# The last block of a mixture-of-experts kernel: four older tiles beside its sum, three tiles moved to the next stretch, additions held back

## The chip, the cores and the metric

The kernel runs on one core of a Trainium2 chip. The metric is the device time of one execution in microseconds (us), here the median of three. A profiled execution gives the trace; its span runs from the first instruction to the last.

## The reference

The input `x` is 16 sequences of 256 positions with 512 channels, 4096 rows in all. There are two layers.

```python
x = x + L0_ffn(L0_cond(x, ...))          # first layer
x = x + L1_ffn(L1_cond(x, cond), Wr, We, be)   # second layer

def L1_cond(x, w):      # a causal convolution of each channel by 16 taps
    return conv(x, w, padding=[(K - 1, 0)], feature_group_count=C)

def L1_ffn(x, Wr, We, be):                # 8 experts, the best two of each row
    w, sel = top_k(x @ Wr, 2)
    w = softmax(w)
    gate = one_hot(sel) weighted by w
    return sum(gate[..., e] * (x @ We[e] + be[e]) for e in range(8))
```

`L0_cond` adds one attended vector for each sequence and normalises; `L0_ffn` is a gated unit of width 2048 with weights and activations rounded to few values.

## The kernel before, in words

The rows are worked in four blocks of 1024 (`NB` = 4), each held as 128 partitions x 8 rows (`PH` = 8) x 512 channels. The first layer, `ffn`, goes through the 32 row groups in order: two products (L444), the gate on ScalarE and VectorE (L449, L450), a rounding (L456 to L462), the downward product (L486), and the sum into the block's tile (L491).

The second layer of a block has three parts:

- `conv` turns the block's channels (L670, copied out at L672) and multiplies them with Toeplitz blocks of the taps (L700), eight chunks of 24 matmul passes; VectorE copies each chunk back (L704). The taps come by L686.
- `route` turns the rows once more (L738, L740), computes the router's logits (L749), picks the best two (L754 to L768), ranks the rows of each expert (a matmul at L789) and gives each row a slot in that expert's region of a DRAM table (`slot`). Then, sixteen times, ScalarE makes a payload, the row times its gate (L810); GpSimd copies four numbers behind it (L811: where the result goes, and the gate) and writes the 128 rows to their slots with an indirect DMA (L812, "routed").
- `experts` takes tiles of 128 rows of one expert from that table. For each it loads the rows (L962), turns them on TensorE (L971), copies them out (L974 on ScalarE, or L976 on VectorE once all biases lie on the chip), multiplies with the expert's weights (L1021, eight passes) and adds the gated bias (L1041). The result `ye` goes out by GpSimd.

There are 71 tiles. A tile is full of one expert's rows, so blocks don't own tiles: after the routing of block n, the tiles that are surely full may run. Tiles 0 to 40 (`S_KEEP` = 41) hold rows of blocks 0 to 2 alone. Tiles 41 to 54 (`S_PURE` = 55) may hold rows of the last block and of older ones, tiles 55 to 70 rows of the last block alone.

Results leave in two ways. An *addition* (L935) is an indirect DMA that adds 128 rows into the output in DRAM; `Adds` makes each wait until the one before has landed. Results that are needed by the last block are instead *kept*: an indirect DMA writes them to the DRAM buffer `kept` (L1045). At the end `total` loads the last block's first-layer result (`x1`, L1069) and the two halves of `kept` (`y_kept`, L1075), adds them on VectorE (L1080) and writes the output (L1082). The `kept` loads wait for all kept writes.

The parts are generators, and `together` interleaves their steps in proportion to weights; a scheduler then sets each engine's order, largely by that order and by what is ready. GpSimd's queue takes indirect DMAs in order, and an instruction that waits holds all that follow.

The last pass of the main loop (n = 4) has an order of its own. Three tiles run with the first layer's last steps, with two result buffers in the pool `moe`. Then the first layer's memory is released and the pool `tail` takes its place: all biases (L1118), 10 tap buffers, 4 payload buffers, 6 row buffers and 6 result buffers. The last convolution and routing run beside tiles 28 to 40, and after them tiles 41 to 70 with a buffer pair of eight results each (`late_y`) for the first fourteen. `total` follows.

```python
                wanted = (s - s0 + 1) % 3 > 0 or s + 1 == s1
                left = 0 if s + 1 == s1 else max(len(held) - 1, 0)
            else:
                wanted, left = True, s + 1 < s1
```

These lines at the end of a tile say which held results are added now: before the last stage all but one, in the last stage two after three tiles.

Of the kernel before, what the change touches and what calls it, by code (L numbers as in the profile page):

```python
# [44 lines left out]
P = 128  # L45
# [10 lines left out]
def adaln_ffn_kernel(ctx: ExitStack, tc: tile.TileContext, t: dict, out: bass.AP):  # L56
# [27 lines left out]
    S_KEEP = TOP * PH * (NB - 1) - (NE - 1)  # L84
    S_PURE = TOP * PH * (NB - 1) + NE - 1
    RS = NT + P

# [573 lines left out]

    def conv(n, banks, pool, ahead):

# [15 lines left out]
        def load_taps(c):  # L679
            taps[c] = []  # L680
            for g in range(c * G4, (c + 1) * G4):
                taps[c].append(
                    pools[pool].tile([P, LAGS, P], F32, tag="taps", bufs=ahead, name="taps")
                    if c > 0 else conv_p.tile([P, LAGS, P], F32, tag="taps", bufs=5, name="taps")
                )
                nc.sync.dma_start(out=taps[c][-1], in_=t["toep"][:, g])  # L686
# [41 lines left out]

    def route(n, pool, pays):

# [74 lines left out]
        for p in range(PH):  # L805
            if p == PH // 2:
                tabs[n + 1] = tabulate(rhs)
            for i in range(TOP):
                pay = pools[pool].tile([P, ROW], F32, tag="pay", bufs=pays, name="pay")
                nc.scalar.activation(pay[:, 0:C], cv[:, p, :], AF.Identity, scale=ends[:, i, p, TOP + 1 : ROW - C])  # L810
                nc.gpsimd.tensor_copy(pay[:, C:ROW], ends[:, i, p, :])  # L811
                routings.append(nc.gpsimd.indirect_dma_start(  # L812
                    out=next(rv), out_offset=bass.IndirectOffsetOnAxis(ap=slot[:, i, p : p + 1], axis=0),
                    in_=pay[:, :], in_offset=None,
                ))
                yield
# [129 lines left out]

    def experts(s0, s1, tab, rows_in, written, pool, ahead, results):


        keeping = s0 >= S_KEEP  # L950
        why = "the table holds rows and experts of its own making"
        pool = pools[pool]
        got = {}
        held = []

# [11 lines left out]
        def turn(s):  # L967
# [4 lines left out]
            xT = moe.tile([P, KC, P], F32, tag="xT", name="xT")  # L972
            if biases is None:
                nc.scalar.copy(xT, xT_ps)  # L974
            else:
                nc.vector.tensor_copy(xT, xT_ps)  # L976
# [3 lines left out]
            if s < S_PURE:  # L980
# [3 lines left out]
                )  # L984
            if keeping:
                spare = part_no[:, 2 + s - s0 : 3 + s - s0]
                nc.vector.tensor_scalar(oi[:, 1:2], ends[:, TOP : TOP + 1], spare, None, ALU.min)
# [12 lines left out]

        for s in range(s0, min(s0 + ahead, s1)):
            load(s)
        turn(s0)
        yield
        late_y = None
        for s in range(s0, s1):
            if s + ahead < s1:
                load(s + ahead)
            if biases is None:
                load_bias(s)  # L1010
            if s + 1 < s1:
                turn(s + 1)
            yield
# [6 lines left out]
            for k in range(KC):  # L1020
# [4 lines left out]
                if k == 1:  # L1025
                    yield
            if keeping and s < S_PURE:
                if (s - s0) % PH == 0:
                    late_y = xp.tile([P, PH, C], F32, tag="x", name="late_y")
                ye = late_y[:, (s - s0) % PH, :]  # L1030
            else:
                ye = pool.tile([P, C], F32, tag="ye", bufs=results, name="ye")
# [9 lines left out]
            if s < S_PURE:  # L1042
                held.append((ye, oi))
            if keeping:
                keeps.append(nc.gpsimd.indirect_dma_start(  # L1045
                    out=next(keep_v), out_offset=bass.IndirectOffsetOnAxis(ap=oi[:, 1:2], axis=0),
                    in_=ye, in_offset=None,
                ))

                wanted = (s - s0 + 1) % 3 > 0 or s + 1 == s1  # L1050
                left = 0 if s + 1 == s1 else max(len(held) - 1, 0)
            else:
                wanted, left = True, s + 1 < s1
            while wanted and len(held) > left:
                y, i = held.pop(0)
                adds(y, i[:, 0:1], last_mm, *rows_in)
                rows_in = []
            yield

    def steps(s0, s1):  # L1060
        return 1 + 3 * (s1 - s0)

    def total():

        x1 = []
        for p in range(PH):
            tag, bufs = ("xg", 6) if p < 6 else ("pay", 4)
            x1.append(tail.tile([P, ROW], F32, tag=tag, bufs=bufs, name="x1")[:, 0:C])
            nc.sync.dma_start(out=x1[p], in_=x1_d[:, p, :])  # L1069
        halves = []  # L1070
        for i in range(TOP):
            halves.append(xp.tile([P, PH, C], F32, tag="x", name="y_kept"))
            rows = from_kept[i * P * PH : (i + 1) * P * PH, :].rearrange("(u p) c -> u p c", p=PH)
            for p in range(0, PH, 2):
                d = nc.sync.dma_start(out=halves[i][:, p : p + 2, :], in_=rows[:, p : p + 2, :])  # L1075
                for it in keeps:
                    tc.add_manual_dep(d.ins, it.ins.name, sync, reason="all results are there")
        for half in halves:
            for p in range(PH):
                nc.vector.tensor_tensor(x1[p], x1[p], half[:, p, :], ALU.add)  # L1080
                if half is halves[-1]:
                    nc.scalar.dma_start(out=out_x1_v[NB - 1][:, p, :], in_=x1[p])  # L1082

    def behind(n, banks, pool, pays, ahead):
        yield from conv(n, banks, pool, ahead)
        yield from route(n, pool, pays)
        if n + 2 < NB:
            load_x(n + 2, nc.sync)

    behind_steps = CONV_STEPS + ROUTE_STEPS  # L1090
    pools = {"moe": moe, "conv": conv_p}
    biases = None
    done = 0
    moe_steps, moe_part = 0, None
    for n in range(1, NB + 1):
        if n < NB:

            streams = [(behind_steps * 7 // 4, behind(n - 1, ps_c, "conv", 2, 5))]
            streams.append((STEPS, part(first_layer, STEPS)))
# [5 lines left out]
        else:  # L1105

            now = done + 3
            rest = behind(n - 1, ps_mm, "tail", 4, 10)
            next(rest)
            first = experts(done, now, tab, rows_in, written, "moe", 3, 2)  # L1110
            together((AHEAD, first_layer), (steps(done, now), first))
            done = now
            work.release()
# [8 lines left out]

            moe_steps, moe_part = steps(done, S_KEEP), experts(done, S_KEEP, tab, rows_in, written, "tail", 6, 6)
            done = S_KEEP
            head = CONV_STEPS + 1 + PH + 1
            for _ in range(2):
                next(rest)
            together((head - 4, part(rest, head - 4)), (3, part(moe_part, 3)))
            together((behind_steps - head, rest), ((moe_steps - 3) * 3 // 2, moe_part))
        end = NS if n == NB else TOP * PH * n - (NE - 1)  # L1130
        moe_steps, tab = steps(done, end), tabs[n]
        rows_in, written = list(stored[: PH // 2 * n]), list(routings)
        if n == NB - 1:
            continue
        moe_part = experts(done, end, tab, rows_in, written, *(("tail", 6, 6) if n == NB else ("moe", 3, 2)))
        done = end
    for _ in moe_part:
        pass
    total()


# [88 lines left out]
```

## Time and profile before

| | us |
|---|---|
| median of three runs | 1042.35 (1041.06 to 1042.97) |
| the profiled execution, its time | 1042.35 |
| its span | 1040.6 |
| TensorE busy in the span | 892.0 (86%) |
| VectorE, ScalarE, GpSimd busy | 582.0, 464.7, 330.0 |
| mean granted TensorE clock | 0.944 |

The shares are averages over stretches with different limits, so the last 270 us are read piece by piece: the first layer ends at 769, the last convolution at 819, the routed writes run from 850 to 881, tiles 41 to 70 from 891 to 1018, and the sum from 1021 on. In the lists of instructions a row gives start, duration, engine, line, operation, output and inputs, a count, and in brackets how long the engine had been idle and what ended that.

### The profile page before, as it was taken

How to read it: one execution, taken by the hardware profiler on the slowest of the kernel's cores; microseconds unless marked ns; L12 is line 12 of the kernel's file. 1: busy time of each engine (PE TensorE's matmuls, PEld its weight loads, DVE VectorE, ACT ScalarE, POOL GpSimd, SP SyncE). 2: the span in 40 equal slices, each digit the busy share in tenths (PEclk: the TensorE clock that was granted, in tenths of full speed). 3: DMA queues.
4: the chain of work that ended last, by engine and by line, in shares of the span. 5: the costliest groups of instructions: out<-in, count | busy, mean ns of one | idle time of the engine just before them, and what ended most of it. 6: DMA issues, size and time to landing. Idle time of an engine off the chain costs nothing.

```text
span 1040.6 us, 13445 instructions
## 1 busy us (share of the span) xinstructions
PE 892.0 (86%) x4456; PEld 503.3 (48%) x4456; DVE 582.0 (56%) x1274; ACT 464.7 (45%) x588; POOL 330.0 (32%) x407
## 2 busy tenths in 40 slices
PE   3687999699988799988798999879997999899890
PEld 1333443367743357653344766434546864344440
DVE  3899764876565966454578453734522353444244
ACT  3697764573587754456564515554521122000000
POOL 0245200632055221025524121452221037244550
PEclk9789998899999899999999999989998989899896
DMA  9961002855125134334431653354378358667676
GB/s 329 363 237 36 24 21 79 281 173 162 31 102 183 52 108 146 92 92 143 152 92 24 192 163 62 112 159 115 79 202 268 82 149 233 160 141 188 159 210 262
DMA packets 71932, 152.35 MB, mean 146 GB/s; under 512 B 9324, under 2 KB 26092, under 8 KB 71224
## 3 DMA queue, kind: packets, MB, share of 16 engines
q1 hardware_dynamic: 52440, 99.23, 29.2%
q0 software_dynamic: 17616, 47.59, 18.8%
q10 hardware_dynamic: 1808, 4.68, 1.3%
q8 instruction: 36, 0.59, 0.2%
q14 instruction: 32, 0.26, 0.1%
HBM read 97.29 MB, written 54.18 MB: 146 GB/s over the span
## 4 chain that ended last, share of the span: by engine, by line
PE 43%; DMA 15%; DVE 13%; ACT 11%; issue 10%; POOL 6%; SPq 1%; DVEq 0%; ACTq 0%; POOLq 0%
PE acc_ps L1021 12%; PE acc_ps L444 9%; PE acc_ps L700 7%; DMA routed<-pay,slot 5%; PE acc_ps L486 4%; DMA out<-late_y,oi 3%; PE acc_ps L749 3%; ACT hq L456 3%; DVE h L450 2%; PE acc_ps L971 2%; ACT hq L462 2%; DMA xt<-in_x 2%; PE acc_ps L738 1%; ACT pay L810 1%; ACT hqT L476 1%
## 5 line engine op out<-in xcount | busy, mean ns | idle before, releaser
L1021 PE MATMUL acc_ps<-we,xT 128*128 x568 | 271.6, 614 | 7.1 <-DVE xT L976 6.7
L444 PEld LDWEIGHTS <-qT 128*128 128x128 bf16 x1024 | 99.7, 99 | 153.0 <-issue 50.2
L450 DVE SCALAR_TENSOR_TENSOR h<-acc_ps,c,h 128x512 f32<-128x512 f32 x128 | 95.2, 746 | 120.4 <-PE acc_ps L444 66.9
L1021 PEld LDWEIGHTS acc_ps<-we,xT 128*128 128x128 f32 x568 | 107.1, 198 | 109.6 <-issue 95.4
L444 PE MATMUL acc_ps<-w2q,qT 128*128 128x512 fp8e4 x512 | 135.9, 387 | 16.1 <-DVE h L450 9.3
L444 PE MATMUL acc_ps<-w1q,qT 128*128 128x512 fp8e4 x512 | 135.5, 383 | 9.8 <-ACT h L449 5.5
L486 PE MATMUL acc_ps<-w3q,hqT 128*128 128x512 fp8e4 x512 | 127.3, 399 | 10.3 <-ACT hqT L476 4.9
L935 POOL DMA_INDIRECT out<-ye,oi x41 | 65.8, 1606 | 208.0 <-PE acc_ps L1021 140.4
L449 ACT ACTIVATE h<-acc_ps,c 128x512 f32<-128x512 f32 x128 | 86.3, 681 | 91.8 <-PE acc_ps L444 91.3
L700 PE MATMUL acc_ps<-taps,xT 128*128 128x128 f32 x768 | 95.9, 282 | 12.4 <-DVE ye L1041 5.5
L700 PEld LDWEIGHTS acc_ps<-taps,xT 128*128 128x128 f32 x768 | 91.2, 196 | 15.8 <-DVE ye L1041 5.7
L486 PEld LDWEIGHTS <-hqT 128*128 128x128 bf16 x512 | 51.4, 102 | 77.4 <-issue 21.7
L812 POOL DMA_INDIRECT routed<-pay,slot x64 | 67.3, 1052 | 48.0 <-ACT pay L810 15.3
L462 ACT ACTIVATE hq<-h,neg_magic 128x2048 bf16<-128x2048 f32 x32 | 64.1, 2002 | 34.4 <-DVE h L461 31.8
L458 DVE TENSOR_REDUCE hmx<-h 128x1 f32<-128x2048 f32 x32 | 73.0, 2282 | 0.6
L810 ACT ACTIVATE pay<-xt,ends 128x512 f32<-128x512 f32 x64 | 45.5, 721 | 58.4 <-DMA routed<-pay,slot 56.1
L456 ACT ACTIVATE hq<-h 128x2048 bf16<-128x2048 f32 x32 | 61.2, 1912 | 20.0 <-DVE h L450 19.8
L476 ACT COPY hqT<-acc_ps 128x1024 bf16<-128x1024 bf16 x64 | 61.6, 1009 | 15.4 <-PE acc_ps L474 11.8
L390 POOL TENSOR_TENSOR y<-xt,pb 128x512 f32<-128x512 f32 x30 | 42.3, 1428 | 54.6 <-ACT q L418 37.3
L1041 DVE SCALAR_TENSOR_TENSOR ye<-biases,xe,acc_ps 128x512 f32<-128x512 f32 x29 | 21.7, 747 | 67.8 <-PE acc_ps L1021 37.3
L704 DVE COPY xt<-acc_ps 128x512 f32<-128x512 f32 x32 | 32.6, 1030 | 39.8 <-PE acc_ps L700 39.8
L971 PEld LDWEIGHTS acc_ps<-ident,xg 128*128 128x128 f32 x284 | 36.0, 147 | 35.4 <-issue 24.1
(194 smaller groups left out, 1112.6 us busy)
## 6 DMA issues: line engine op xcount, KB each, us to landing
taps<-in_toep SPq DMA_DIRECT2D x128, 192.0 KB
xg<-routed SPq DMA_DIRECT2D x71, 258.0 KB
xt<-in_x SPq DMA_DIRECT2D x16, 512.0 KB
we<-in_We POOLq DMA_DIRECT2D x8, 1024.0 KB
bias<-in_be SPq DMA_DIRECT2D x28, 256.0 KB
out<-xt SPq DMA_DIRECT2D x12, 512.0 KB
st<-in_w1T SPq DMA_DIRECT2D x4, 1024.0 KB
st<-in_w2T SPq DMA_DIRECT2D x4, 1024.0 KB
```

The costliest lines, as they stand in the source:

```text
L444: nc.tensor.matmul(acc[-1], lhsT=qTs[i][:, k, bass.ts(j, P)], rhs=wq[:, k, bass.ts(f, 512)], start=(k == 0), stop=(k == KC - 1),)
L449: marks["silu", m] = nc.scalar.activation(h, acc[0], AF.Silu, scale=c1[:, j : j + 1])
L450: marks["glu", m] = nc.vector.scalar_tensor_tensor(h, acc[1], c2[:, j : j + 1], h, ALU.mult, ALU.mult)
L456: nc.scalar.activation(hq, h, AF.Square, accum_out=hss)
L458: nc.vector.tensor_reduce(hmx, h, AX.X, ALU.max, apply_absolute_value=True)
L462: nc.scalar.activation(hq, h, AF.Identity, bias=neg_magic)
L476: nc.scalar.copy(hqT, hT_ps)
L486: nc.tensor.matmul(o_ps, lhsT=hqT[k // half][:, k % half, :], rhs=w3q[:, k, :], start=(k == 0), stop=(k == KF - 1),)
L700: nc.tensor.matmul(cv_ps[:, g, :], lhsT=xT[:, g, at : at + P], rhs=mine[g][:, lag, :], start=(lag == 0), stop=(lag == LAGS - 1),)
L812: routings.append(nc.gpsimd.indirect_dma_start(out=next(rv), out_offset=bass.IndirectOffsetOnAxis(ap=slot[:, i, p : p + 1], axis=0), in_=p ...
L935: d = nc.gpsimd.indirect_dma_start(out=next(add_v), out_offset=bass.IndirectOffsetOnAxis(ap=idx, axis=0), in_=ye, in_offset=None, compute_ ...
L1021: last_mm = nc.tensor.matmul(e_ps, lhsT=xT[:, k, :], rhs=we[:, bass.ds(e, 1), k, :].rearrange("p o f -> p (o f)"), start=(k == 0), stop=(k ...
```

## The change

Tiles get an order list (`seq`) instead of a range, and `S_LAST` = `S_KEEP` - 4 = 37.

- Block 2's time in the first layer has 13 tiles (9 to 21) instead of 16; the three beside the first layer's end are 22 to 24; the last routing has 25 to 36; the last stage has 41 to 70 and then 37 to 40.
- `total` becomes a generator. It is started after tile 70, and its sum is interleaved with what is left of the four older tiles, whose additions come last. The output is written from SP's queue instead of ScalarE's.
- The list of held results is shared by all calls. In the last routing the results of tiles 31 to 36 are held, and added in the last stage, two after three tiles as before.
- In the last routing, the convolution and the logits come before tile 25's matmuls in the written order, with only that tile's rows turned ahead; before, one tile was interleaved with them and the following ones ran with a larger weight.
- Taps, payloads and `x1` of the last block share 12 buffers. The four numbers behind a payload are copied by ScalarE in the last routing. The turned rows are copied by ScalarE in the last stage. The biases of the three tiles at the first layer's end are loaded a tile earlier.

```diff
+    S_LAST = S_KEEP - 4
...
+    def row_of_tail(name):
+        return pools["tail"].tile([P, ROW], F32, tag="row", bufs=12, name=name)
...
-                nc.gpsimd.tensor_copy(pay[:, C:ROW], ends[:, i, p, :])
+                if pool == "tail":
+                    nc.scalar.copy(pay[:, C:ROW], ends[:, i, p, :])
+                else:
+                    nc.gpsimd.tensor_copy(pay[:, C:ROW], ends[:, i, p, :])
...
-    def experts(s0, s1, tab, rows_in, written, pool, ahead, results):
+    held = []
+    def experts(seq, tab, rows_in, written, pool, ahead, results):
...
-            if biases is None:
+            if biases is None or seq[0] >= S_KEEP:
                 nc.scalar.copy(xT, xT_ps)
...
-            if s + 1 < s1:
-                turn(s + 1)
+            for ready in seq[i + 1 : i + 2]:
+                turn(ready)
+                if biases is None and len(seq) == 3:
+                    load_bias(ready)
...
-                wanted = (s - s0 + 1) % 3 > 0 or s + 1 == s1
-                left = 0 if s + 1 == s1 else max(len(held) - 1, 0)
+                wanted = (s - S_KEEP + 1) % 3 > 0 or s + 1 == NS
+                left = 0 if s + 1 == NS else max(len(held) - 1, 0)
+            elif s >= S_LAST:
+                wanted, left = True, 0
             else:
-                wanted, left = True, s + 1 < s1
+                wanted, left = s < S_LAST - results, s not in (seq[-1], S_LAST - results - 1)
...
     def total():
...
+        yield
         for half in halves:
             for p in range(PH):
                 nc.vector.tensor_tensor(x1[p], x1[p], half[:, p, :], ALU.add)
                 if half is halves[-1]:
-                    nc.scalar.dma_start(out=out_x1_v[NB - 1][:, p, :], in_=x1[p])
+                    nc.sync.dma_start(out=out_x1_v[NB - 1][:, p, :], in_=x1[p])
+                if p % 2:
+                    yield
...
-            now = done + 3
+            first = [done + i for i in range(3)]
...
-            moe_steps, moe_part = steps(done, S_KEEP), experts(done, S_KEEP, tab, rows_in, written, "tail", 6, 6)
-            done = S_KEEP
+            moe_steps, moe_part = steps(seq), experts(seq, tab, rows_in, written, "tail", 6, 6)
             head = CONV_STEPS + 1 + PH + 1
             for _ in range(2):
                 next(rest)
-            together((head - 4, part(rest, head - 4)), (3, part(moe_part, 3)))
-            together((behind_steps - head, rest), ((moe_steps - 3) * 3 // 2, moe_part))
+            next(moe_part)
+            for _ in range(head - 4):
+                next(rest)
+            together((behind_steps - head, rest), (moe_steps - 1, moe_part))
...
+            end = TOP * PH * n - (NE - 1) - (3 if n == NB - 2 else 0)
...
-    for _ in moe_part:
-        pass
-    total()
+    seq = [*range(S_KEEP, NS), *range(S_LAST, S_KEEP)]
+    moe_part = experts(seq, tab, rows_in, written, "tail", 6, 6)
+    for _ in range(steps(range(S_KEEP, NS))):
+        next(moe_part)
+    last_sum = total()
+    next(last_sum)
+    for _ in range(7):
+        next(moe_part)
+    together((PH, last_sum), (steps(range(S_LAST, S_KEEP)) - 7, moe_part))
```

## Prediction, made before the changed kernel ran

> **What bounds the kernel now.** I read the page's slices, then busy time in stretches cut where the last block changes its work, then the queues of GpSimd (POOL) and VectorE (DVE) in order of time, and last the chain of waits. A tile is one pass of `experts`, 0 to 70. The stretches (length; busy us and instructions of PE, PEld, DVE, ACT, POOL; clock; DMA share; GB/s):
>
> ```profile
> 740.00:770.00 30.00, 30.00 (x136) 14.97 (x135) 12.69 (x25) 11.56 (x13) 7.74 (x8) 1.00 0.49 109
> 770.00:801.00 31.00, 23.64 (x134) 16.77 (x132) 4.00 (x10) 4.49 (x8) 4.67 (x3) 0.99 0.96 306
> 850.00:881.00 31.00, 31.00 (x99) 15.55 (x98) 16.30 (x60) 8.62 (x12) 24.06 (x32) 1.00 0.88 259
> 974.00:1018.00 44.00, 38.50 (x106) 17.92 (x104) 14.63 (x32) 0.00 (x0) 23.47 (x22) 0.92 0.66 177
> 1025.00:1031.00 6.00, 0.00 (x0) 0.00 (x0) 5.94 (x10) 0.00 (x0) 0.00 (x0) 0.50 1.00 393
> ```
>
> TensorE (PE) bounds the first layer's end, is idle for 7.4 us at the start of the last convolution and 5.5 us late in the last stage, and has nothing in the final 22 us, where the DMA engines are full. The timeline shows the idle time at the convolution:
>
> ```profile
> 782.99 0.75 DVE L1041 SCALAR_TENSOR_TENSOR ye<-bias,xe,acc_ps 128x512 f32<-128x512 f32 x1 [8.84 <-DMA out<-ye,oi]
> 791.01 0.75 DVE L1041 SCALAR_TENSOR_TENSOR ye<-bias,xe,acc_ps 128x512 f32<-128x512 f32 x1 [7.28 <-DMA out<-ye,oi]
> 800.33 0.75 DVE L1041 SCALAR_TENSOR_TENSOR ye<-bias,xe,acc_ps 128x512 f32<-128x512 f32 x1 [7.79 <-DMA out<-ye,oi]
> 801.13 5.49 PE L700 MATMUL acc_ps<-taps,xT 128*128 128x128 f32 x24 [5.48 <-DVE ye L1041]
> ```
>
> Results of tiles 25, 26 and 27 wait for a free one of two buffers, that is for an addition (L935) to land; behind them on DVE stand the convolution's copies (L704), and PE waits for their banks. The end of the chain of waits:
>
> ```profile
> 974.03 5.68 DMA out<-late_y,oi
> 980.48 2.86 DMA out<-late_y,oi
> 987.86 4.80 DMA kept<-ye,oi
> 1017.84 2.71 DMA kept<-ye,oi
> 1020.82 4.01 DMA y_kept<-kept
> ```
>
> Additions run one by one; the kept writes (L1045) queue behind them on POOL, tiles wait for buffers that those writes hold, and after the last kept write come its landing, the loads of `y_kept` and the sum.
>
> **The change, part by part** (span 1040.6 us; the profiled run took 1042.35, so 1.75 lies outside; that is also the median). Positions are from the built queues of both kernels.
>
> *First layer.* Before its last L486, PE's queue holds 24.5 tiles now and 22 after. A tile costs 3.87 us (four L971 at 0.44 in all, eight L1021 at 3.44). PE is busy for 68.4 of 700 to 770, but 32.6 of the 40 us before it, where half a tile also leaves. I take 2 tiles, **-8** (bounds 0 and 2.5 x 3.87 = -9.7). Call E the moment of the last L491, 768.90 now, 760.9 after.
>
> *Additions and the convolution.* The wait for buffers stays: tile 24 will need addition 22, as tile 27 needs addition 25. An addition is queued after the next tile's last matmul, and its buffer is free when it lands. Counting matmuls back from E in the new queue, addition 18 can go at E-15, and 19 and 20 follow at 7.3 us (766.37 to 773.69), so 20 goes at E-0.4; at 8.1 (the mean of the five gaps from 766.37 to 806.82, while the DMA engines are full) 21 goes at E+7.7 and 22 at E+15.8, which lands near E+24. Now tile 27 comes at E+31.4. So the convolution's copies come **-7** nearer to E (0 if DMA bounds this stretch; -9, which is 5.5 and 1.6 idle and 2 of slow clock after it). The bias that tile 23 needs is queued ahead of the taps instead of among them; now the taps stand behind such a bias from 769.9 to 774.10. PE ends its tiles at E+11.7 and three chunks (2.7 and 0.4 of transposes each) by E+21, so this wait remains the last. The last convolution matmul moves from 818.9 to about 803.9.
>
> *Logits to the first routed write.* PE has 3.25 tiles between convolution and rank matmul (L789), 2.5 after: 0.75 x 3.87, **-2.9** (0 to -3.9).
>
> *The sixteen routed writes.* Four additions stand between the first and the last of them, now and after: what is held back is tiles 31 to 36, not these. Their gaps are 6.6 to 7.4 us (853.98, 860.56, 867.70, 875.05), longer than three writes and an addition (3 x 1.28 + 1.9 = 5.7). So the four-element copies moved from POOL to ACT (0.2 us each, on an ACT queue with 22 us free in 31) shorten nothing: **0** (-3, POOL bound; +1). Nor do the twelve shared row buffers: ACT waited 8.1 us (at 854.19) for one of four, but POOL never more than 1.2 in this stage. On SP four loads of the sum's first operand now stand ahead of tile 41's rows; their buffers come free with the payloads of writes 4 to 7, before the last write, which those rows await anyway: 0.
>
> *Start of the last stage.* Tile 36 ends at 885.2 - 15 - 3.87 = 866 (tile 40 now ends at 885.2; after the convolution 12 tiles follow instead of 13), the first rows land at 887.07 - 17.9 = 869, so PE idles again. Now 3.9 us pass from landing (887.07) to the matmul (890.95), since DVE first does two old results. ACT does the copy in the new order, free of them: about 1.6 (transposes and a copy of 0.58 by L974). **-2.3** (0 to -4).
>
> *Thirty tiles.* Tile 41's result to tile 70's took 897.13 to 1016.82, 119.7, against 29 x 3.87 = 112.2. The 7.5 lost are waits for kept writes behind additions. The new queue spreads two additions over three kept writes up to the last: 11.4 us (5.72 each, 922.63 to 996.96) against 11.6 of tiles. I take **-6** (0 to -7.5).
>
> *The end.* From the last kept write, K, 22.8 us passed to the end (1017.84 to 1040.6). Now four tiles run there and four additions close POOL's queue. Tile 37's result comes 3.6 us after K (3.87 after tile 70's, and 0.75 long), and each addition waits for the one before. DMA share is 1.00 to K+18, so I price the first two at that 8.1, the third at 7, the last at 5.7, landing within: 3.6+8.1+8.1+7+5.7 = 32.5, say 32: **+9.2**. Bounds: all at 5.7 behind DVE's results, 27.5 (+4.7); all at 9.1 (773.69 to 801.03), 40 (+17). On DVE the result of tile 38 stands behind three sums that wait for `y_kept` (K+7 and 2 us), and those of 39 and 40 behind six and five more; they are ready by K+20, before their additions' turns. SP takes the output's eight issues at 0.33, behind loads that are done: nothing.
>
> The Trainium skill ("DMA: Bandwidth & Descriptors", Anatomy of one DMA) gives a GpSimd DMA about 2 us and its bytes at 436 GB/s, 2.6 us for an addition's 256 KB by my estimate. By it four additions would hide beside the sum, and the end would cost nothing. The same page (Issuing engines are not separate DMA queues) speaks against the change: all issuers share the same engines. By bytes alone, 1 MB at 400 GB/s adds an estimated 2.6 us. The trace's spacing of 5.72 and more decides against both.
>
> Sum: -8 -7 -2.9 +0 -2.3 -6 +9.2 = -17.0; span 1023.6, time 1025.4.
>
> **Rivals.**
>
> *DMA bounds the convolution.* In 770 to 801 the share is 0.96 at 306 GB/s, 9.5 MB of biases, taps and rows, and the same bytes move after. Then the term of -7 is 0: 1032.4. Against: PE waited for taps only 0.3 us there.
>
> *Additions pace the last stage (slower).* Between the last routed write and the last kept write stand 21 additions, and each now also stands behind kept writes that wait for tiles. At 5.72 they take 120 us from about 862 and end 8 us before the tiles, so they decide from 5.72 + 8/21 = 6.1 on, and cost 21 us per us beyond. At 6.8 (mean of the routed stage) the last kept write is 15 later: 1040, no change; at 7.35 (its longest) 26 later: 1051.5. From 6.9 on it is slower than now. For it: the two paces differ by 0.2 us in 11.6. Against: the same neighbours gave 5.72.
>
> *The end stays short.* If the additions run at 5.72 there, +4.7 replaces +9.2: 1020.9.
>
> *It does not do what it says.* The additions between routed writes stay four; that is in the sum at nothing.
>
> **Numbers.** The sum's case 0.58, short end 0.12, DMA-bound convolution 0.17, pacing additions 0.13 (of which 0.09 beyond 1044.4, 0.03 near no change and 0.01 below). About 0.2% (2.1 us) is what a measurement can tell here. So faster 0.58 + 0.12 + 0.17 + 0.01 = 0.88, less 0.01 to the same side for a near miss: 0.87; same 0.04; slower 0.09. Term errors of about 4, 4.5, 2, 2, 2, 3 and 6 give some 10 about 1025.4; with the DMA case the range runs from 1013 to 1038, leaving out the pacing case and a stroke of luck in all terms.
>
> **What would show it.** Right: last L491 near 761; tile 24's result near 785 after a wait for an addition; last convolution matmul near 804 (818.9 now); first routed write near 832, last near 862; L974 on ACT in the last stage; last kept write near 992 with additions 5.7 apart; four additions 6 to 8 us apart after it, the last thing to land. Wrong: the additions' spacing over 6.1 in the last stage, PE waiting for taps, or a chain that ends with the output's writes and not with an addition.

## The result, and the profile after

Over twenty timed executions of each kernel the changed one has a median of 1037.26 us and the one before 1042.61 us. The ratio is 0.9946, with a 95% interval of 0.9927 to 0.9965: faster by 5.6 us, between 3.6 and 7.6. The forecast was 17. The profiled execution of the changed kernel took 1038.07 us, its span 1036.3 (before 1042.35 and 1040.6).

I read the stretches first (length; busy us and instructions of PE, PEld, DVE, ACT, POOL; clock; DMA share; GB/s). Lines of the changed kernel are numbered a little higher: L492 is the sum behind the downward product (L491 before), L1035 the tile's matmuls, L1055 its result, L947 the addition, L1059 the kept write, L1097 the sum.

```profile
740.00:770.00 30.00, 29.75 (x136) 15.15 (x134) 12.56 (x25) 12.05 (x14) 7.10 (x6) 1.00 0.55 123
770.00:801.00 31.00, 21.96 (x129) 16.99 (x128) 6.64 (x13) 3.41 (x6) 5.52 (x6) 0.94 0.96 297
881.00:1001.00 120.00, 120.00 (x370) 59.05 (x369) 37.94 (x109) 18.40 (x32) 59.58 (x49) 0.99 0.75 181
1001.00:1036.00 35.00, 12.14 (x35) 5.48 (x33) 12.92 (x22) 1.17 (x2) 8.38 (x6) 0.71 0.75 231
```

The last stage is now full: PE is busy for all of 120 us. The stretch at the convolution is not better but a little worse: 22.0 us of PE in 31 instead of 23.6, at the same DMA share of 0.96. The timeline of that stretch (start, duration, engine, line, and in brackets idle time and what ended it) shows why:

```profile
765.57 1.56 POOL L947 DMA_INDIRECT out<-ye,oi  x1 [5.10 <-DVE ye L1055]
779.87 1.55 POOL L947 DMA_INDIRECT out<-ye,oi  x1 [12.74 <-PE acc_ps L675]
787.11 1.56 POOL L947 DMA_INDIRECT out<-ye,oi  x1 [4.98 <-DVE ye L1055]
794.59 0.75 DVE L1055 SCALAR_TENSOR_TENSOR ye<-bias,xe,acc_ps 128x512 f32<-128x512 f32 x1 [4.78 <-DMA taps<-in_toep]
795.28 1.55 POOL L947 DMA_INDIRECT out<-ye,oi  x1 [6.61 <-DMA out<-ye,oi]
```

With E the last L492 (766.31), addition 20 goes at E-0.7, as forecast (E-0.4). Then comes a gap of 14.3 us where the sum had 8.1, and tile 24's result comes at E+28.3 instead of E+24. The label "taps" on that result is the case of a wait for several semaphores: its buffer came free when the addition of 787.11 landed, for which the next addition waited too (last line). What PE waited for between 755 and 815, and what held SP's queue before it issued the next taps (what waits, for what: us, times, longest):

```profile
PE acc_ps L675 <- DVE xT L988: 5.6, 1, 5.6
PE acc_ps L983 <- DMA xg<-routed: 3.2, 1, 3.2
SPq L692 <- DMA biases<-in_be: 6.8, 1, 6.8
```

The 5.6 us are VectorE's queue: a copy of turned rows stands there behind tile 24's result and two of the convolution's copies. The 3.2 us are rows that came late. They are issued on SP's queue behind the taps, and that queue stood still for 6.8 us, until the 2 MB load of all biases had landed (for 5.0 us in the kernel before, where PE waited for no rows).

The end of the chain of waits, and below it the additions behind the last kept write (1001.50):

```profile
1001.50 3.06 DMA kept<-ye,oi
1004.96 6.56 DMA y_kept<-kept
1012.16 0.74 DVE ye L1055
1021.11 5.70 DMA out<-ye,oi
```

```profile
1003.68 1.60 POOL L947 DMA_INDIRECT out<-ye,oi  x1 [1.22 <-DVE oi L994]
1013.18 1.75 POOL L947 DMA_INDIRECT out<-ye,oi  x1 [7.90 <-DVE ye L1055]
1021.11 2.34 POOL L947 DMA_INDIRECT out<-ye,oi  x1 [6.19 <-DVE ye L1055]
1027.56 1.54 POOL L947 DMA_INDIRECT out<-ye,oi  x1 [4.11 <-DMA out<-ye,oi]
```

Where before the chain ended with `y_kept`, the sum and the output, it now ends with additions. One thing in these two traces misleads. Up to the twentieth of the 32 downward sums the queues of both kernels hold the same order, yet the changed kernel reached that point at 493.0 and the one before at 488.5. Fourteen experiments and one more trace of the kernel before gave more traces of most stages, since each experiment leaves most of the order as it is. So the stages can be compared by means. A row takes the traces whose experiment leaves its stage as it is; the run with the 2 MB load in small pieces is in none (in the stages that it leaves alone it would widen no range by more than 0.1 us), and the run that holds no results back is not in the last two (its end took 35.8).

| stage | before, 2 traces | changed order (range; traces) | measured | forecast |
|---|---|---|---|---|
| start to 20th downward sum | 491.1 | 491.6 (488.5 to 495.1; 12) | +0.5 | 0 |
| to the last downward sum, E | 280.3 | 274.5 (272.1 to 278.2; 12) | -5.8 | -8 |
| to the last convolution matmul | 49.0 | 48.3 (46.0 to 50.6; 7) | -0.7 | -7 |
| to the first routed write | 29.3 | 25.6 (24.0 to 28.1; 7) | -3.7 | -2.9 |
| to the last routed write | 29.7 | 31.4 (30.6 to 31.9; 7) | +1.7 | 0 |
| to the last kept write, K | 139.0 | 128.5 (127.6 to 129.3; 6) | -10.5 | -8.3 |
| to the end | 22.6 | 34.5 (34.2 to 34.9; 6) | +12.0 | +9.2 |

The stages behind the first row sum to -7.0, which the interval of the timings (-7.6 to -3.6) holds. Two rows make most of the missing ten: the convolution (6.3) and the end (2.8). The two traces of before lie 3.6 us apart in the row to the first routed write and 2 us apart in the rows to the last convolution matmul and to K, so these rows are uncertain by about as much; the convolution's -0.7 can't be told from nothing.

### The profile page after: what moved, and what is told of

It reads as the page before. It is cut to its first block, busy times and chain, and to the rows that moved or that the text cites. A ratio compares the mean times of both kernels' runs of the same rounds, so it can differ in the third digit from the quotient of the medians.

```text
span 1036.3 us, 13485 instructions
## 1 busy us (share of the span) xinstructions
PE 886.6 (86%) x4456; PEld 501.1 (48%) x4456; DVE 568.0 (55%) x1243; ACT 484.1 (47%) x635; POOL 326.5 (32%) x391
## 4 chain that ended last, share of the span: by engine, by line
PE 50%; DVE 13%; DMA 12%; ACT 10%; issue 8%; POOL 6%; SPq 1%; DVEq 0%; POOLq 0%; ACTq 0%
PE acc_ps L1035 18%; PE acc_ps L445 9%; PE acc_ps L706 7%; DMA routed<-pay,slot 5%; PE acc_ps L487 5%; PE acc_ps L755 3%; PE acc_ps L983 3%; ACT hq L457 2%; DVE h L451 2%; DMA taps<-in_toep 2%; DMA xt<-in_x 2%; ACT hq L463 2%; POOL r L131 1%; PE acc_ps L744 1%; POOL y L391 1%
## 5 line engine op out<-in xcount | busy, mean ns | idle before, releaser
L1035 PE MATMUL acc_ps<-we,xT 128*128 x568 | 264.6, 602 | 1.6 <-ACT h L450 1.4
L1035 PEld LDWEIGHTS acc_ps<-we,xT 128*128 128x128 f32 x568 | 104.5, 193 | 99.5 <-issue 92.6
L487 PE MATMUL acc_ps<-w3q,hqT 128*128 128x512 fp8e4 x512 | 130.9, 408 | 9.7 <-ACT hqT L477 4.8
L947 POOL DMA_INDIRECT out<-ye,oi x41 | 66.1, 1613 | 218.2 <-PE acc_ps L1035 124.7
L986 ACT COPY xT<-acc_ps 128x512 f32<-128x512 f32 x59 | 34.4, 585 | 160.5 <-PE acc_ps L983 146.9
L706 PEld LDWEIGHTS acc_ps<-taps,xT 128*128 128x128 f32 x768 | 90.3, 195 | 10.1 <-issue 2.2
L391 POOL TENSOR_TENSOR y<-xt,pb 128x512 f32<-128x512 f32 x30 | 42.3, 1427 | 54.4 <-ACT q L419 36.4
L1055 DVE SCALAR_TENSOR_TENSOR ye<-biases,xe,acc_ps 128x512 f32<-128x512 f32 x32 | 23.9, 747 | 63.2 <-PE acc_ps L1035 58.3
```

What stands on the lines that cost most here:

```text
L487: nc.tensor.matmul(o_ps, lhsT=hqT[k // half][:, k % half, :], rhs=w3q[:, k, :], start=(k == 0), stop=(k == KF - 1),)
L706: nc.tensor.matmul(cv_ps[:, g, :], lhsT=xT[:, g, at : at + P], rhs=mine[g][:, lag, :], start=(lag == 0), stop=(lag == LAGS - 1),)
L947: d = nc.gpsimd.indirect_dma_start(out=next(add_v), out_offset=bass.IndirectOffsetOnAxis(ap=idx, axis=0), in_=ye, in_offset=None, compute_ ...
L1035: last_mm = nc.tensor.matmul(e_ps, lhsT=xT[:, k, :], rhs=we[:, bass.ds(e, 1), k, :].rearrange("p o f -> p (o f)"), start=(k == 0), stop=(k ...
```

## The experiments

Each was timed beside the kernel before; the changed kernel stands at 0.9946 on that scale. 0.001 is 1.04 us. A difference between two such ratios is uncertain by some 3 to 4 us, so the traces decide about stages, and the ratios about large effects only.

**Own result buffers at the convolution.** Two of the three tiles take payload buffers that are idle there.

```diff
-                ye = pool.tile([P, C], F32, tag="ye", bufs=results, name="ye")
+                if len(seq) == 3 and i < 2:
+                    ye = conv_p.tile([P, ROW], F32, tag="pay", bufs=2, name="ye")[:, 0:C]
+                else:
+                    ye = pool.tile([P, C], F32, tag="ye", bufs=results, name="ye")
```

> Two of the three tiles beside the first layer's end get result buffers of their own, so none of their results waits for an addition that is still under way; the same bytes move. Theory (additions bound the start of the last convolution, as predicted, and one of them took 13.6 us there): the result of tile 24 comes about 14 us after the last L492 instead of 28.3, PE's idle time before the convolution's banks goes, the last convolution matmul comes 5 to 8 us nearer to the last L492 than the 48.6 us of the changed kernel, and the time falls by about 5 us. Rival (the DMA bytes of biases, taps and rows bound this stretch): PE waits for taps or rows instead, the last convolution matmul stays within 2 us of 48.6, the time within 1 us.

Ratio 0.9916 [0.9887, 0.9946], 3 us under the changed kernel. The convolution ends at E+44.5. VectorE's timeline around it, E being 762.61, and what PE waited for:

```profile
767.35 0.75 DVE L1058 SCALAR_TENSOR_TENSOR ye<-bias,xe,acc_ps 128x512 f32<-128x512 f32 x1 [3.99 <-PE acc_ps L1035]
771.22 0.75 DVE L1058 SCALAR_TENSOR_TENSOR ye<-bias,xe,acc_ps 128x512 f32<-128x512 f32 x1 [3.12 <-PE acc_ps L1035]
785.58 0.17 DVE L990 COPY xe<-xg 128x4 f32<-128x4 f32 x1 [13.61 <-DMA xg<-routed]
786.49 0.74 DVE L1058 SCALAR_TENSOR_TENSOR ye<-bias,xe,acc_ps 128x512 f32<-128x512 f32 x1
```

```profile
PE acc_ps L983 <- DMA xg<-routed: 3.8, 1, 3.8
```

Two results now follow PE at once. The third, tile 24's, stands on VectorE behind a small copy of tile 25's first row data, whose load came late, at E+23. That is neither the theory's E+14 nor the rival's unchanged convolution. So additions were the last wait, as the prediction said, but a second one lay just 4 us under it: rows that stand on SP's queue behind the taps and the 2 MB load (SP waits 6.7 us for that load here too).

**The 2 MB load of biases later.** It is issued behind half of the convolution, by a dependency on that copy.

```diff
-            nc.scalar.dma_start(
-                out=biases.rearrange("p e c -> p (e c)"),
...
             for _ in range(head - 4):
                 next(rest)
+            d = nc.scalar.dma_start(
+                out=biases.rearrange("p e c -> p (e c)"),
...
+            tc.add_manual_dep(d.ins, copied[-4].ins.name, sync, reason="after half of the convolution")
```

> The 2 MB load of all biases is issued behind half of the last convolution instead of ahead of it (some taps then stand behind rows on SP's queue); the bytes in all are the same. Theory (that load, beside the taps, is what stretches one addition to 13.3 to 13.8 us in all five traces): this addition takes 7 to 9 us, tile 24's result comes about 22 us after the last L492 instead of 28, the last convolution matmul 3 to 6 us sooner, time -4. Rival (taps and rows alone fill the DMA engines): the addition still takes 12 us or more, tile 24 stays at 27 to 29, time within 1.5 us.

Ratio 0.9902 [0.9863, 0.9941]; the convolution ends at E+43.8. The gap behind addition 20 is 8.8 us, instead of 13.5 to 14.3 in the nine traces that have the changed order there and the load in its place. PE waits for no rows there either:

```profile
768.22 1.56 POOL L949 DMA_INDIRECT out<-ye,oi  x1 [5.62 <-DVE ye L1057]
777.01 1.55 POOL L949 DMA_INDIRECT out<-ye,oi  x1 [7.22 <-issue]
```

**Taps later, biases in place.** The edit before had also moved some taps on SP's queue, so the taps were tried by themselves.

```diff
-                nc.sync.dma_start(out=taps[c][-1], in_=t["toep"][:, g])
+                d = nc.sync.dma_start(out=taps[c][-1], in_=t["toep"][:, g])
+                if pool == "tail" and c > 0:
+                    order_behind(d, bias_loads[-1])
```

> Of the changed kernel only SP's order at the last convolution: the taps behind the first chunk's are issued after the bias of tile 24, which waits for a buffer; the 2 MB load of all biases stays at the end of the first layer. The late load of the biases had also moved half of ten taps behind that bias, so it did not tell which of the two stretched the addition issued 0.4 us before the last L492. Theory A (the 2 MB of biases do): it takes 12 us or more again. Theory B (it is the burst of taps): 7 to 9 us, though the taps come later. Either way PE may wait for taps, so the time is open: -4 to +4.

Ratio 0.9954 [0.993, 0.9978]. The gap is 13.8 us again:

```profile
762.08 1.56 POOL L949 DMA_INDIRECT out<-ye,oi  x1 [5.16 <-DVE ye L1060]
775.90 1.55 POOL L949 DMA_INDIRECT out<-ye,oi  x1 [12.26 <-PE acc_ps L675]
```

So the 2 MB load stretches that addition, not the burst of taps. The load hangs on E in both kernels and begins within 0.1 us of it; what moved is the additions. In the kernel before, this load began at 768.94, 2.6 us after one addition (766.37) and 4.8 us ahead of the next (773.69), and the gaps behind them were 7.3 and 10.0. In the changed order it begins 0.3 to 0.8 us after the addition in all nine traces. The DMA queues between 755 and 815 in the changed kernel (packets, MB, share of 16 engines) let one suspect the size of its packets:

```profile
q1 hardware_dynamic: 6192, 9.72, 50.5%
q0 software_dynamic: 937, 1.69, 18.2%
q10 hardware_dynamic: 144, 2.10, 9.3%
```

q10 holds the biases, 14.6 KB a packet on average; q0 the indirect DMAs, 1.8 KB. The Trainium skill ("DMA: Bandwidth & Descriptors", Queues, rings and completion order) has each DMA engine take turns between queues by whole packets, which would make a small packet wait for a large one each time.

**The same load in small pieces.**

```diff
-            nc.scalar.dma_start(
-                out=biases.rearrange("p e c -> p (e c)"),
...
+            for e in range(NE):
+                nc.scalar.dma_start(out=biases[:, e, :], in_=t["be"][e, :].partition_broadcast(P))
```

> Of the changed kernel only the form of the 2 MB load: eight DMAs of 256 KB, one per expert, instead of one; they start at the same place (the second to seventh behind ScalarE's copy for tile 23). In the trace of the changed kernel this load goes in 144 packets of 14.6 KB (2.10 MB / 144), the additions in packets of 1.8 KB (1.69 MB / 937). Theory P (the addition shares each DMA engine with that load turn by turn, a packet each, and each of its small packets waits for a large one): the addition issued 0.4 us before the last L492 takes 8 to 10 us instead of 13.6, tile 24's result comes 4 us sooner, the last convolution matmul 44 to 45 us after the last L492, time -4, though the same bytes move. Theory B (the bytes themselves hold it up): 12 us or more, convolution 47 to 50, time unchanged.

The load went in 1152 packets of 1.8 KB, the gap was 11.2 us, tile 24 came at E+27.4, the convolution ended at E+46.4; ratio 0.9922 [0.9884, 0.9961]. That is between the two theories. But three of the eight pieces were issued only at E+10.3, E+11.7 and E+14.1, when tile 23's result (E+10.1) had shown that the addition was down, so fewer bytes met it as well. What the packets and what the bytes contribute to the five us stays open, and the rule about turns is neither refuted nor shown.

**The end: results ahead of the sums.** All four older tiles' results stand before the first sum on VectorE.

```diff
+                a = nc.vector.tensor_tensor(x1[p], x1[p], half[:, p, :], ALU.add)
+                tc.add_manual_dep(a.ins, made[-1].ins.name, in_turn, reason="an engine's order")
```

> On VectorE the four older tiles' results stand ahead of all sixteen sums; nothing else moves. Theory (the final additions wait in part for results that stand behind sums): the second addition comes about 2 us and the fourth about 2 us sooner, and from the last kept write to the end pass 31 to 33 us instead of 34.8, time -2 to -3. Rival (each addition is only as slow as the full DMA engines make it): 34 to 35 us, time unchanged; the sums end some 8 us later and still before the last addition lands.

Both were wrong: ratio 0.9987 [0.9959, 1.0016], 4 us slower than the changed kernel, and 38.7 us from K to the end. In the timeline the third addition took GpSimd 5.49 us to issue instead of 1.6, from 1019.56 until just behind the last of sixteen sums in a row:

```profile
1013.92 9.72 DVE L1099 TENSOR_TENSOR x<-x,y_kept 128x512 f32<-128x512 f32 x16
1019.56 5.49 POOL L947 DMA_INDIRECT out<-ye,oi  x1 [5.40 <-DVE x L1099]
```

With the results in between, the two middle issues take 1.75 and 2.34 us. The Trainium skill ("SBUF — State Buffer", SBUF: two separate sides) has VectorE and GpSimd share one port pair under an exclusive lock, so that a DMA issued by GpSimd cannot get its descriptors written while VectorE runs an operation in a two-port mode; an operation with two inputs in SBUF, as the sum is, takes the pair only against GpSimd operations that read SBUF. The issue of 5.49 us would fit. Another row does not: in the changed kernel the issue at 1013.18 took 1.75 us beside six sums without a break:

```profile
1012.82 3.69 DVE L1097 TENSOR_TENSOR x<-x,y_kept 128x512 f32<-128x512 f32 x6
```

So sums beside it do not stretch every issue. That this order costs 4 us is measured; why the one issue took so long stays open.

**The end without its additions.**

```diff
             elif s >= S_LAST:
-                wanted, left = True, 0
+                wanted, left = False, 0
```

> The additions of tiles 37 to 40 are left out (their rows of the output lack them); the tiles themselves still run. Theory (the four additions end the kernel): from the last kept write to the end pass about 24 us instead of 34.8, near the 22.8 of the kernel before, time -10. Rival (the tiles' matmuls and results and the delayed sums hold the end too): 28 us or more, time -6 or less.

Ratio 0.983 [0.9797, 0.9863], 12 us under the changed kernel; K to the end is 22.1 us. All of the +12.0 is the additions; the tiles and the mixed sums cost nothing.

**Fewer older tiles at the end.** `S_LAST = S_KEEP` (none), then `S_KEEP - 3`.

> Tiles 37 to 40 go back into the last routing; the rest of the change stays. Theory: four tiles of 3.87 us stand again before tile 41, less the 3.8 us that PE idles there now, so the last kept write comes 11 to 12 us later, and the end takes 22 to 24 us instead of 34.8: the two cancel, time within 2 us of the changed kernel. Rival 1 (the four tiles at the end are what gains): slower than the changed kernel by 5 us or more. Rival 2 (they are what costs): faster by 4 us or more.

Ratio 1.002 [0.9993, 1.0048]: 7.7 us slower, as the first rival had it. From the last routed to the last kept write 148.0 us passed instead of 128.5, and the end took 22.4. So four tiles cost 12 there and save 19.5. That is more than 4 x 3.87, since results of that many tiles wait for their buffers again and PE for the copies behind them on VectorE (waits between 850 and 1030; the changed kernel has neither there):

```profile
DVE ye L1055 <- DMA out<-ye,oi: 27.4, 6, 5.3
PE acc_ps L1035 <- DVE xT L988: 5.0, 3, 2.7
```

> Three older tiles at the end instead of four. Theory (each addition that closes the kernel costs 6.5 to 8 us there and a tile put back ahead of tile 41 costs 19.2 / 4 = 4.8): the last kept write 4 to 5 us later, the end about 27 us instead of 34.8, time -3. Rival (the fourth tile pays like the other three, by the 7.8 us that all four brought): time +2.

Ratio 0.9925 [0.9895, 0.9955], 2 us under the changed kernel by the timings. K did not move (128.2 us after the last routed write), as the tile fits into the 3.9 us in which PE waits for rows there; the end took 29.2 us, 5.3 less.

**The additions held back no longer.**

```diff
-                wanted, left = s < S_LAST - results, s not in (seq[-1], S_LAST - results - 1)
+                wanted, left = True, s != seq[-1]
```

> Of the changed kernel only the holding is undone: the results of tiles 31 to 36 are added as soon as they may, before the last stage's kept writes. Theory (PE bounds the last stage, and 16 late result buffers cover kept writes that come late): first kept write 15 to 20 us later, last kept write within 1.5 us of the changed kernel's 128.3 us after the last routed write, time within 2 us. Rival (held additions are what freed the last stage): the last kept write 4 us or more later, time +4.

The rival was right: ratio 1.0029 [1.0002, 1.0057], 8.6 us slower. The first kept write came 25 us later, the last 6.7 us later after the last routed write (135.2). Beside the rows, PE now waited for ScalarE's copies and for results (engine, line, for what: us, times, longest; 835 to 1045):

```profile
PE acc_ps L1035 <- ACT xT L986: 4.1, 2, 3.4
PE acc_ps L983 <- DMA xg<-routed: 4.1, 1, 4.1
PE acc_ps L1035 <- DVE ye L1055: 3.2, 3, 1.6
```

**The copy in the last stage back on VectorE.**

```diff
-            if biases is None or seq[0] >= S_KEEP:
+            if biases is None:
```

> Of the changed kernel only the copy of the turned rows in the last stage goes back to VectorE, as in the kernel before. Theory (the start of the last stage gains by it, as predicted 2.3): from the last routed write to the last kept write 1.5 to 4 us more than 128.3, the end unchanged within 1 us, time +1 to +4. Rival (VectorE has the time, and the copy was never late): 128 to 129 us, time unchanged.

Ratio 0.9984 [0.9959, 1.0009]; 130.8 us to the last kept write, 2.3 more, the end 34.7. As forecast.

**The kernel before again, and the tiles not moved.** The second edit is `- (3 if n == NB - 2 else 0)` taken out of `end`.

> The kernel before once more, for a second trace of it. Up to the result of the twentieth of the 32 downward products the queues of both kernels are the same, and that point scatters from 488.5 to 495.1 us over six traces. Theory (the first-layer term is real and lies behind that point): from there to the last L491 it takes 279 to 281 us again, against a mean of 274.1 in the five traces of the changed order, so the term is about -6. Rival (the first trace of before was a long one): 277 us or less, and the term is -3 or nothing.

The time of this one execution was 1043.28 us. From the twentieth to the last downward sum 280.2 us (280.4 in the first trace): the first-layer term is real.

> Sixteen tiles instead of thirteen run in the first layer's time again; the four at the end, the held additions and all else stay. Theory (the three tiles lengthen the first layer, and behind it PE has idle time for them): from the twentieth downward product to the last L492 280 us instead of 274, from there to the last kept write 233 to 236 us as now, time +4 to +7. Rival (three tiles less in the last routing shorten that as much): the last kept write comes 5 us or more sooner after the last L492, time within 1.5 us of the changed kernel.

Ratio 0.9991 [0.9963, 1.0019], 4.7 us slower; the first layer took 280.3. But from E to K 228.4 us passed, 5 less than with the move (233.8 by the table), and only two additions stood between the routed writes instead of four: 24.6 us from the first to the last instead of 31.4. The trace hence has the move at nothing, the timings at +4.7.

> The three-edit kernel with sixteen instead of thirteen tiles in the first layer's time. Theory (the move is worth what the first layer gains, since PE has idle time behind it): first layer 280 instead of 275 us from the twentieth downward product, from the last L492 to the last kept write 226 to 228 as with the move, time +4 to +6. Rival (as in the trace without the move, where the last kept write came 6.8 us sooner after the last L492, one addition less standing between the routed writes): 220 us, time within 1.5 us.

Ratio 0.9848 [0.9816, 0.988] against 0.9825 [0.9792, 0.9859] with the move (the next experiment): 2.4 us, inside the uncertainty. First layer 278.9 against 275.2, E to K 223.6 against 227.5, with three additions between the routed writes. What the first layer gains is mostly given back between the routed writes; what is left of it, 0 to 5 us, stays open.

**Three edits together**: own buffers, biases later, three tiles at the end; then with two tiles, where the sum is also written behind the tiles instead of among them.

> Three edits together: own result buffers for two of the three tiles beside the first layer's end, the biases loaded behind half of the last convolution, three older tiles at the end instead of four. Theory (additions and the 2 MB load are two waits in a row at the convolution, one behind the other): last convolution matmul 38 to 42 us after the last L492 (44.5 and 43.8 with one edit, 48 without), the end 29 us, time some 10 us under the changed kernel's, 1.5% under the kernel before. Rival (either edit alone frees all that there is): the convolution stays at 43.5 or more, time -6.

Ratio 0.9825 [0.9792, 0.9859], a median of 1025.05 us: the best version, 1.75% under the kernel before. The convolution ends at E+37.9, so the two edits add up (48.3, less 3.8, less 4.5 would be 40.0), and PE waits there no more than 0.3 us at a time. The end took 29.2.

> As with three older tiles at the end, but with two. Theory (two additions are hidden beside the sum's loads and its output, and the second tile put back ahead of tile 41 costs PE about 5 us, since PE's idle time there took in only the first): the last kept write 4 to 6 us later than with three, the end 23 instead of 29 us, time within 2 us of the three-tile version. Rival (both tiles put back fit into idle time): 5 us faster.

Ratio 0.9848 [0.9815, 0.9881]. The end was 25.0, but K came 138.8 us after the last routed write instead of 130.1, more than either side had expected. Three is as good as two or better.

## Why the prediction was wrong, point by point

The sign was right, and the chain ends with an addition as foreseen. The terms have the forecast signs too, but for the routed writes, which were put at nothing (+1.7), and the convolution, whose -0.7 is no more than scatter. The sizes of two terms were wrong.

*Additions and the convolution, -7 forecast, -0.7 measured: the step that failed.* The queue count was right to 0.4 us: additions 18, 19 and 20 at E-14.9, E-7.4, E-0.7. The failing step is "at 8.1 (the mean of the five gaps ...) 21 goes at E+7.7". A mean gap of before was put on an addition that in the new order meets the start of a 2 MB load. It took 13.5 to 14.3 us; with the load moved it took 8.8, and the convolution came 4.5 us sooner. So tile 24 came at E+28.3, 4.3 us late. After its result PE still waited 3.5 us (to 798.14) behind VectorE's copies, where it had waited 0.8 behind tile 27's result before; the sum had nothing for that. The meeting was visible in the built queues: both the addition and the load hang on E. I had counted the bytes as unchanged and asked whether they bound the stretch as a whole, not which single transfer they would meet. The rival "DMA bounds the convolution" gave the right time for the stretch (1032.4 in all), but half the mechanism: with free buffers, additions no longer counted and rows did, 4 us lower. The 0.3 us that PE waited for taps, set against that rival, belongs to an earlier convolution (617.34); in the last one PE waited for none, before or after.

*First layer, -8 forecast, -5.8 measured, within its bounds.* From 700 to 740 PE is busy for 36.4 us where it was 38.4: part of what left had filled waits. That tiles there are worth less than 3.87 each is argued from this row, not shown by a run of its own. The forecast last L492 (761, found at 766.3) missed mostly by the 4.5 us that this trace lost ahead of any change.

*Logits to first routed write, -2.9 forecast, -3.7 measured; sixteen writes, 0 and +1.7.* Right within their bounds but for 0.7.

*Last stage, -8.3 forecast (-2.3 and -6), -10.5 measured.* The copy is worth 2.3, as forecast. The additions of the last stage came 5.87 us apart (mean of 18 gaps), under the 6.1 from which the slower rival decides; PE waits for nothing there. Holding is worth 6.7 (8.6 by the timings). Ahead of that run I took it for nothing; PE does not bound the stage alone once five more additions stand ahead of its first kept write.

*The end, +9.2 forecast, +12.0 measured.* The sum was 3.6, 8.1, 8.1, 7, 5.7. The trace has 2.2, 9.5, 7.9, 6.5, 8.7. The mis-sized term is the last: I let the final addition take its spacing, "landing within". But from the issue of the last addition 8.4 to 8.7 us pass to the end in all traces with four (9.5 to 9.6 with three). In the changed kernel the last row with any transfer ends at 1032, and 4 us of nothing follow (first line); in the kernel before 2 us did, behind output writes (second line). The DMA share of "1.00 to K+18" that priced the first two holds in the kernel before only from K+6 on.

```profile
1032.00:1034.00 2.00, 0.00 (x0) 0.00 (x0) 0.00 (x0) 0.00 (x0) 0.00 (x0) 0.50 0.00 0
1038.00:1039.00 1.00, 0.00 (x0) 0.00 (x0) 0.00 (x0) 0.00 (x0) 0.00 (x0) 0.50 0.26 98
```

## What to carry to other kernels

A duration that is a mean of several rows holds for the neighbours it had. For each serial transfer that the sum leans on, look in the new queues for what starts within its time, and price it beside that. Where a chain's last link moves to another kind of transfer, count that link to the end of the program, not to the next issue. And before a stage is called won or lost on two traces, subtract a point up to which both kernels are the same: here it moved by 6.6 us without any change.

## What was not expected of the hardware

The scatter comes with the granted clock: over the twenty executions of the changed kernel the longer spans have the lower clocks (correlation -0.81). These executions run from a span of 1028.5 us at a mean clock of 0.956 to one of 1041.0 at 0.937. One place in the two first traces shows how it can arise. The same 163 matmuls took 25 us before (435 to 460) and 27 us after (438 to 465); in both, PE's longest idle time in the middle is the same 1.77 us, and only in the second does the clock then stand at half. Below are two stretches of the kernel before, PE's first row behind that idle time in each kernel, and three stretches of the changed one (columns as above; the clock is the third number from the end):

```profile
450.00:455.00 5.00, 2.97 (x31) 2.59 (x31) 3.10 (x10) 2.50 (x4) 2.33 (x3) 1.00 0.41 52
455.00:460.00 5.00, 4.18 (x28) 2.13 (x26) 4.73 (x21) 3.43 (x4) 0.31 (x2) 1.00 0.02 3
```

```profile
451.97 1.06 PE L749 MATMUL acc_ps<-wr,cvT 128*128 128x8 f32 x8 [1.77 <-ACT cvT L740]
455.07 1.06 PE L755 MATMUL acc_ps<-wr,cvT 128*128 128x8 f32 x8 [1.77 <-ACT cvT L746]
```

```profile
454.00:456.00 2.00, 0.93 (x9) 0.94 (x10) 1.42 (x2) 1.01 (x3) 1.85 (x3) 1.00 0.21 16
456.00:458.00 2.00, 1.94 (x16) 1.67 (x15) 0.63 (x6) 0.58 (x1) 0.06 (x1) 0.56 0.79 115
458.00:460.00 2.00, 2.00 (x13) 1.59 (x13) 1.23 (x4) 0.00 (x0) 0.00 (x0) 0.50 0.00 0
```

The Trainium skill ("TensorE: Matmul & The Clock Gate", What's actually happening) has the clock halved after an idle window of about 3.4 us, counted in windows that run on by themselves, which would let the same gap cost something in one execution and nothing in the next. The two traces agree in that. They do not fit it in the length: here the clock was halved behind an idle time of 1.77 us.

Additions of 256 KB came 5.87 us apart in the last stage, 8.8 beside taps and rows, and 13.8 apart (typically) when a load of 2 MB in large packets began beside the first of them. In one trace GpSimd's issue of one took 5.5 instead of 1.6 us while VectorE added sixteen tiles in a row, for a reason that stays open: order on an engine that has time to spare decided over 4 us at the end.
